# Layer 3's recurrence: the product with B moves into a PSUM bank, directly ahead of the sum that takes it

## The chip, the cores and the metric

The kernel runs on one core of a Trainium2 chip. A core has five engines with an instruction queue each: TensorE (PE; its weight loads are listed as PEld), VectorE (DVE), ScalarE (ACT), GpSimd (POOL) and SyncE (SP), which here issues nearly all transfers. They share the on-chip memory SBUF; PSUM, in eight banks of 128 partitions x 512 floats, takes the products of TensorE, and VectorE and ScalarE read and write it too. Engines wait for each other, and for transfers, on semaphores. The metric is the device time of one execution in microseconds (us), the median of several runs.

## The reference

Four layers follow one another: a four-way Mamba block over 2 x 4096 tokens, two attention layers, and layer 3, a small Mamba block with a group norm. Only layer 3 changes. It cuts the 128 channels of each of the 2 x 4096 pixels into a sequence of 8 tokens of 16 channels, and runs one Mamba block over all the sequences:

```python
xz = seq @ in_proj_w.T                      # seq: (8192, 8, 16) -> 2 x 32 inner channels
xi, z = split(xz);  xs = silu(causal_conv4(xi) + conv_b)
dt, Bm, Cm = split(xs @ x_proj_w.T)         # 1, 16 and 16 columns
dt = softplus(dt @ dt_proj_w.T + dt_proj_b)
dA  = exp(dt[..., None] * A)                # (n, 8, 32, 16)
dBx = dt[..., None] * Bm[:, :, None, :] * xs[..., None]
def step(h, (dA_t, dBx_t, C_t)):
    h = dA_t * h + dBx_t                    # eight steps, one for each token
    return h, einsum('nds,ns->nd', h, C_t)
y = (ys + xs * D) * silu(z);  out = y @ out_proj_w.T
```

A group norm, a SiLU and a residual sum over the picture follow. The line that matters is `h = dA_t * h + dBx_t`: for each token one product with the state and one sum, on 32 x 16 values for each pixel.

## The kernel before

Layers 0 to 2 are the same in both kernels. In layer 3 the pixels are taken in 16 chunks of 512 (`Chunk3`, 8 for each picture). Tokens are taken in pairs: step k = 0 to 3 of a chunk holds the tokens 2k and 2k+1, called o = 0 and 1. The state of one token is a tile of 128 x 4 x 512 floats (32 inner channels x 4 states on the partitions, four groups g of states beside each other), and nearly every operation on it takes a half of it, 128 x 1024 floats. So m01 stands for the product of o = 0, half 1.

For one token and half these operations are made:

- `load` brings B to SBUF, as the tile D, by broadcast from a row tensor in HBM; SP issues it two steps ahead. Six D tiles rotate.
- `rx_` spreads dt * x ("dtx", the tile e) over the partitions with one matmul into a PSUM bank named rx.
- `db_` multiplies D by it in place, on VectorE: D = B dtx. In PLAN this is "D", made for the next step.
- `da_` makes A = exp(dt * A) on ScalarE, one step ahead.
- `mul` (m) multiplies A by the state of the token before, on POOL.
- `add` adds it to D, on VectorE (v) or POOL (g). D then is the state. The first token's state is D alone.
- `hc_` (C) multiplies A by the spread of C, which `pc_` put into a PSUM bank q with two matmuls (two q tiles of two banks each), on VectorE, for the step before; `y_` sums it over the states on TensorE, into the bank y. The share of B dtx in C h is made apart, by `cbx_` and `ecb_`; `yg_` is the gating.
- `time` makes the step size and dtx of the next chunk, two POOL operations.

The order of the work is written out by hand. The loop runs over steps s, and in each over four groups. `PLAN[k][g]` lists the operations of a group, in the order in which each engine gets its own; `prepare` issues the `pc_` of the following C at the head of a group that has a C, `y_` and the entries of `first` come next, and the entries of `extra` behind the plan's. Every engine takes its instructions in the order in which they are issued here. Before the change both `rx_` of a step are entries of `extra`, at the end of the step two ahead, into two banks.

A chunk has 14 m, 14 D, 8 v, 4 g and 14 C. In PSUM, layer 3 holds the banks misc (1), rx (2), q (4) and y (1).

Of the kernel before, what the change touches and what calls it, by code (L numbers as in the profile page):

```python
# [7 lines left out]
F32 = mybir.dt.float32  # L8
# [5 lines left out]
P = 128  # L14
B, C, H, W = 2, 128, 64, 64
L = H * W
T = 512
# [34 lines left out]
def _bc(ap, axis, shape):  # L52
    return ap.unsqueeze(axis).to_broadcast(shape)
# [3 lines left out]
def conv_seq_kernel(ctx: ExitStack, tc: tile.TileContext, a: dict, out: bass.AP):  # L57
    nc = tc.nc
# [8 lines left out]
    x = gt([P, B, L], "x")  # L67
# [30 lines left out]
    with ExitStack() as c0:  # L98
# [3 lines left out]
        ps = c0.enter_context(tc.tile_pool(name="ps0", bufs=1, space=PSUM))  # L102
# [380 lines left out]
        nk = len(chunks)  # L483
# [12 lines left out]
        with tc.manual_schedule():  # L496
            c, c1 = chunks[:2]
# [113 lines left out]
            for k, c in enumerate(chunks):  # L611
# [8 lines left out]
                A, V, M, G = {}, {}, {}, {}  # L620
# [191 lines left out]
    with ExitStack() as c1:  # L812
# [7 lines left out]
        ps = c1.enter_context(tc.tile_pool(name="ps1", bufs=1, space=PSUM, reuse_waits="tile"))  # L820
# [301 lines left out]
        for n, j in enumerate(jobs):  # L1122
# [67 lines left out]
        with tc.manual_schedule():  # L1190
# [22 lines left out]
            for slot in range((len(groups) + 2) * UPG):  # L1213
                u = slot % UPG
                G = at(slot)[0]
# [5 lines left out]
                G, d = at(slot - 1)  # L1221
# [4 lines left out]
                G = at(slot - UPG)[0]  # L1226
# [34 lines left out]
    with ExitStack() as c3:  # L1261
# [15 lines left out]
        class Chunk3:  # L1277
# [104 lines left out]
            def rx_(self, k, o):  # L1382

                if k == 3 and o:
                    return
                i, j = PLACE[k]
                r = slice(32 * (j + o), 32 * (j + o) + 32)
                q = self.rx[k, o] = ps.tile([P, T], F32, tag="rx", name="rx", bufs=2)
                mm(q, lhsT=rep[r, :], rhs=self.e[r, i, :], start=True, stop=True)

            def db_(self, k, o, half):
                d = self.D[k, o][:, 2 * half : 2 * half + 2, :]
                nc.vector.tensor_mul(d, d, _bc(self.rx[k, o], 1, [P, 2, T]))

            def da_(self, k):

# [12 lines left out]
                a_ = self.A[k, o][:, g, :]  # L1409
                nc.gpsimd.tensor_mul(a_, a_, h)  # L1410

            def add(self, k, o, half, eng):
                g = slice(2 * half, 2 * half + 2)
                d = self.D[k, o][:, g, :]
                eng.tensor_add(d, d, self.A[k, o][:, g, :])  # L1415

            def unit(self, k, u):

# [105 lines left out]
        def prepare():  # L1524
# [8 lines left out]


        PLAN = (
# [4 lines left out]
        )  # L1540


        y = ps.tile([P, T], F32, tag="y", name="y")

        with tc.manual_schedule():
# [3 lines left out]
            c.spread(0)  # L1549
            for o in range(2):  # L1550
                c.load(0, o)
            for o in range(2):
                c.rx_(0, o)
            c1.xs = xs1
            c1.dt_(0)
            norms = [Norm(b) for b in range(B)]
            for s in range(-1, len(steps) + 3):
# [12 lines left out]
                def more(key, *what, at=extra):  # L1570
                    at.setdefault(key, []).extend(what)
# [28 lines left out]
                if n2 is not None:  # L1600
                    more((k, 0), lambda: n2.spread(n2k), lambda: n2.load(n2k, 0))
                    more((k, 1), lambda: n2.load(n2k, 1))
                    more((k, 3), lambda: n2.rx_(n2k, 0), lambda: n2.rx_(n2k, 1))
                if ci == NCH:
                    more((3, 2), nrm.first)
                    more((3, 3), nrm.second, nrm.third)
# [8 lines left out]
                        more(at_, lambda j=j: nrm.store(j, (G, V)[j % 2]))  # L1615

                nd = 0
                for g in range(4):
                    ops = PLAN[k][g].split()
                    if pc_ is None:  # L1620
                        ops = [o for o in ops if o != "C"]
                    if nc_ is None:
                        ops = [o for o in ops if o != "D"]
                    if cc is None:
                        ops = [o for o in ops if o[0] not in "mvg"]
                    if "C" in ops:
                        prepare()


                    if pc_ is not None and pk and g:  # L1630
                        pc_.y_(pk, g - 1)
                    (older, ok) = at(s - 2)
                    if g == 0 and older is not None and ok:
                        older.y_(ok, 3)
                    for f_ in first.get((k, g), []):
                        f_()
                    if g == 0 and nc_ is not None:
                        nc_.da_(nk)
                    for o in ops:
                        if o == "C":  # L1640
                            c_, k_, u_ = cs[used]
                            c_.hc_(k_, u_)
                            used += 1
                        elif o == "D":
                            nc_.db_(nk, nd // 2, nd % 2)
                            nd += 1
                        elif o == "time":
                            if fut is not None:
                                fut.dt_add()
                                fut.dtx_()  # L1650
                        elif o[0] == "m":
                            cc.mul(ck, int(o[1]), int(o[2]))
                        else:
                            cc.add(ck, int(o[1]), int(o[2]), V if o[0] == "v" else G)
                    for f_ in extra.get((k, g), []):
                        f_()
                if s < 0:
# [120 lines left out]
```

## Time and profile before

| what | value |
|---|---|
| median of three runs | 6480.78 us (6466.40 to 6482.95) |
| the profiled execution | 6465.86 us, span 6464.1 us |
| VectorE / POOL / TensorE / ScalarE busy | 5684.0 / 5442.7 / 5753.8 / 4459.6 us |
| layer 3, 5700 to 6464 us | VectorE 709.7, POOL 635.6, TensorE 657.0, ScalarE 363.1 us |
| VectorE's sum of layer 3 (L1415), 128 of them | 2298 ns each |
| POOL's product (L1410), 224, and sum (L1415), 64 | 2370 and 2895 ns each |
| VectorE's product B dtx (L1393), 224 | 1210 ns each |

The page counts an instruction as busy from its start to its end, so that an instruction that started and could not get on is busy too. A profiled group is written as line, engine, operation, out<-in, shape and count. In a timeline the columns are start, length, engine, line and operation, "x2" means that two follow each other directly, and the idle time before it stands in brackets, with the instruction or transfer that ended it. TensorE's matmuls in float32 are recorded in passes, so that one pair of `pc_` shows as four records, and their ends are modelled.

### The profile page before, as it was taken

To read this page: it belongs to the slowest core of one execution; us is meant where nothing else is said; L and a number is where in the kernel's file an instruction comes from. 1 tells how busy PE (TensorE), PEld (TensorE's weight loads), DVE (VectorE), ACT (ScalarE), POOL (GpSimd) and SP (SyncE) were. 2 spreads that over 40 slices of the span, in tenths; PEclk is the share of its full clock that TensorE was granted. 3 is DMA by queue.
4 is the path that set the end of the run, shared out by engine and by line. 5 is a ranking of instruction groups with operands and counts; after the bars stand their busy time and mean duration, and the time that the engine had idled before them with its cause. 6 is when DMAs were issued, how large, how long until landed. Compare 5 with 4: busy or idle time off the path is not lost.

```text
span 6464.1 us, 66100 instructions
## 1 busy us (share of the span) xinstructions
PE 5753.8 (89%) x19758; PEld 2749.6 (43%) x19758; DVE 5684.0 (88%) x4604; ACT 4459.6 (69%) x7643; POOL 5442.7 (84%) x2543
## 2 busy tenths in 40 slices
PE   8888888888888888888888999999999999888897
PEld 2222222222222222222224888888888888222222
DVE  7999999999999999999998777777777777899998
ACT  7887778877788777888776566556556565554543
POOL 6999999999999999999997677666766566788887
PEclk8888787877778777887777999999999999789888
DMA  6566665566665656665662000000000000877775
GB/s 183 144 152 162 162 154 145 144 150 150 150 151 148 151 148 148 145 150 151 149 147 66 1 5 3 1 1 1 1 1 1 2 6 7 204 177 178 185 181 130
DMA packets 400474, 700.32 MB, mean 108 GB/s; under 512 B 74089, under 2 KB 76658, under 8 KB 399730
## 3 DMA queue, kind: packets, MB, share of 16 engines
q1 hardware_dynamic: 399232, 694.33, 43.9%
q8 instruction: 155, 2.54, 0.2%
q14 instruction: 205, 1.68, 0.1%
q10 hardware_dynamic: 882, 1.78, 0.1%
HBM read 584.53 MB, written 111.28 MB: 108 GB/s over the span
## 4 chain that ended last, share of the span: by engine, by line
PE 39%; POOL 16%; DMA 14%; DVE 11%; ACT 10%; issue 8%; SPq 3%; POOLq 0%; DVEq 0%; ACTq 0%
PE s L961 13%; PE av L1016 12%; POOL dbu L383 9%; DVE h L427 4%; DMA D<-rows 4%; POOL hc L437 3%; DMA dus<-ddu 3%; ACT da L396 3%; PE misc L281 2%; DVE hc L439 2%; DMA cs<-rows 2%; DMA dts<-ddt 2%; PE y L450 2%; PE misc L1076 1%; DVE D L1415 1%
## 5 line engine op out<-in xcount | busy, mean ns | idle before, releaser
L383 POOL TENSOR_TENSOR dbu<-dus,bs 128x1024 f32<-128x1024 f32 x1024 | 2461.5, 2441 | 104.9 <-DVE h L427 87.2
L427 DVE TENSOR_TENSOR_SCAN h<-da,hst,dbu 128x1024 f32<-128x1024 f32 x896 | 2094.6, 2345 | 95.5 <-ACT dbu L411 87.7
L396 ACT ACTIVATE da<-dts,aneg 128x512 f32<-128x512 f32 (+1 forms) x2048 | 1410.4, 689 | 352.4 <-DVE h L427 313.7
L1004 POOL TENSOR_TENSOR sum<-sum,sc 128x1024 f32<-128x1024 f32 x378 | 897.6, 2375 | 397.2 <-ACT sc L999 392.4
L966 ACT COPY sc<-s 128x512 f32<-128x512 f32 x1024 | 596.9, 585 | 704.2 <-PE s L961 576.3
L961 PE MATMUL s<-q,k 128*128 128x256 f32 x4096 | 1053.9, 380 | 10.0 <-ACT lo L919 5.5
L450 PE MATMUL y<-hc,cst 128*32 128x512 f32 x4096 | 877.0, 753 | 207.8 <-DVE hc L439 187.8
L1016 PE MATMUL av<-sc,v 128*128 128x256 f32 x4096 | 1051.1, 380 | 9.1 <-ACT sc L999 9.1
L973 DVE TENSOR_TENSOR mx<-mx,s 128x512 f32<-128x512 f32 x896 | 609.9, 681 | 370.3 <-ACT sc L966 362.6
L439 DVE TENSOR_TENSOR hc<-h,pc 128x1024 f32<-128x1024 f32 x704 | 845.3, 1201 | 10.3 <-PE y L450 8.4
L961 PEld LDWEIGHTS s<-q,k 128*128 128x128 f32 x4096 | 772.3, 191 | 124.5 <-issue 8.3
L1016 PEld LDWEIGHTS av<-sc,v 128*128 128x128 f32 x4096 | 772.7, 190 | 116.4 <-ACT sc L999 14.4
L437 POOL TENSOR_TENSOR hc<-h,cs 128x1024 f32<-128x1024 f32 x320 | 763.1, 2385 | 1.1 <-issue 1.1
L416 PE MATMUL pc<-xd,sel 16*128 16x512 f32 x1024 | 707.0, 781 | 0.1
L1410 POOL TENSOR_TENSOR A<-A,D 128x1024 f32<-128x1024 f32 x224 | 526.6, 2370 | 139.6 <-DVE D L1415 109.8
L996 DVE TENSOR_TENSOR sc<-sc,pm 128x1024 f32<-128x1024 f32 x512 | 620.7, 1212 | 1.7 <-PE pm L991 1.7
L999 ACT ACTIVATE sc<-sc 128x1024 f32<-128x1024 f32 x512 | 543.3, 1061 | 43.3 <-DVE sc L996 43.1
L340 PE MATMUL misc<-xd,w_dt 9*128 9x512 f32 x504 | 369.9, 821 | 143.9 <-ACT x L479 77.1
L450 PEld LDWEIGHTS y<-hc,cst 128*32 128x32 f32 x4096 | 125.2, 120 | 863.2 <-DVE hc L439 427.3
L411 ACT ACTIVATE dbu<-hst,dbu,df 128x1 f32<-128x1 f32 x896 | 337.9, 377 | 84.3 <-POOL dbu L383 61.8
L1427 PE MATMUL q<-xs,room 32*128 32x512 f32 x840 | 283.5, 687 | 70.3 <-DVE A L1433 69.1
L416 PEld LDWEIGHTS pc<-xd,sel 16*128 16x128 f32 x1024 | 182.3, 218 | 350.6 <-issue 303.2
(315 smaller groups left out, 7728.0 us busy)
## 6 DMA issues: line engine op xcount, KB each, us to landing
dts<-ddt SPq DMA_DIRECT2D x512, 256.0 KB, 5.4
dus<-ddu SPq DMA_DIRECT2D x512, 256.0 KB, 5.0
D<-rows SPq DMA_DIRECT2D x448, 256.0 KB, 5.9
bs<-rows SPq DMA_DIRECT2D x1024, 64.0 KB, 4.9
cs<-rows SPq DMA_DIRECT2D x1024, 64.0 KB, 3.2
ddt<-dt SPq DMA_DIRECT2D x128, 256.0 KB, 2.0
ddu<-dtu SPq DMA_DIRECT2D x128, 256.0 KB, 4.0
dtr<-ddt SPq DMA_DIRECT2D x448, 64.0 KB, 2.0
```

The lines of the kernel that those rows point to most:

```text
L383: nc.gpsimd.tensor_mul(t, self.dus[q], _bc(self.bs[g], 1, [P, 2, T]))
L396: act(t[:, i, sl], self.dts[q][:, i, sl], AF.Exp, scale=an[:, g, 2 * q + i : 2 * q + i + 1])
L416: mm(t, lhsT=sel[32:48, 4 * g : 4 * g + 4, :].rearrange("p n d -> p (n d)"), rhs=self.xd[32:48, :], start=True, stop=True)
L427: nc.vector.tensor_tensor_scan(ho, ai, bi, init, ALU.mult, ALU.add)
L437: nc.gpsimd.tensor_mul(t, self.h[u], _bc(self.cs[gq(u)[0]], 1, [P, 2, T]))
L439: nc.vector.tensor_mul(t, self.h[u], _bc(self.pc[u // 2], 1, [P, 2, T]))
L450: mm(self.y[q // 2][r : r + 32, :], lhsT=sum4, rhs=self.hc[u][:, i, :], start=False, stop=(u % 8 >= 6), skip_group_check=True)
L961: mm(p[:, o, :], lhsT=j.k[m // 8][:, m % 8 * P : m % 8 * P + P], rhs=self.q, start=True, stop=True)
L973: nc.vector.tensor_max(self.mx, self.s[0][:, 0:2, :] if u == 1 else self.mx, self.p[u])
L996: nc.vector.tensor_sub(s, s, _bc(self.pm[:, :], 1, [P, 4, NQ]))
L1004: self.adds.tensor_add(self.sum, self.s[0] if w == 1 else self.sum, self.s[w])
L1016: mm(self.av, lhsT=self.job.v[m // 8][:, m % 8, :], rhs=self.s[u // 2][:, m % 4, :], start=(m == 0), stop=(m == 31))
```

## The change

Eight of the fourteen B dtx products of a chunk leave their place one step ahead. In the new `fuse` (x in PLAN) VectorE makes the product for one group of 512 columns into a new PSUM bank "dd", and then the sum, which takes it from there and A from SBUF and writes D; this twice for a half. The fuse stands where v stood. Of the six other products, the four whose sum is POOL's (d) now stand in the same step, directly behind x10 (in step 3: at the head of the second group), and the two of the first token stay one step ahead (D).

rx has one bank in place of two; the other one is dd. A table `RX` gives for each rx matmul the step and group at whose head, behind `prepare` and `y_`, it is issued.

```diff
-                q = self.rx[k, o] = ps.tile([P, T], F32, tag="rx", name="rx", bufs=2)
+                q = self.rx[k, o] = ps.tile([P, T], F32, tag="rx", name="rx")
...
+            def fuse(self, k, o, half):
+                d, a_ = self.D[k, o], self.A[k, o]
+                for g in (2 * half, 2 * half + 1):
+                    t = ps.tile([P, T], F32, tag="dd", name="dd")
+                    nc.vector.tensor_mul(t, d[:, g, :], self.rx[k, o])
+                    nc.vector.tensor_add(d[:, g, :], t, a_[:, g, :])
...
         PLAN = (
-            ("m10 m11 C D", "C D time", "C v10 D", "g11 D C"),
-            ("m00 m01 C D v00", "C v01 D m10 m11", "v10 D", "g11 D"),
-            ("m00 m01 C D v00", "C v01 m10 m11", "C v10 D", "g11 C"),
-            ("m00 m01 C D", "C v00 D g01 m10 m11", "C D", "D C"),
+            ("m10 m11 C", "x10 d11 C", "time C", "g11 C"),
+            ("m00 m01 C x00", "x01 m10 m11 C", "x10 d11", "g11"),
+            ("m00 m01 C x00", "x01 m10 m11 C", "C x10 d11", "C g11"),
+            ("m00 m01 C x00", "d01 g01 m10 m11 C", "C D", "D C"),
         )
+        RX = {(0, 0): (0, 1), (0, 3): (1, 0), (1, 2): (1, 1), (1, 3): (2, 0), (2, 2): (2, 1),
+              (2, 3): (3, 0), (3, 2): (0, 0)}
...
-            for o in range(2):
-                c.rx_(0, o)
...
-                    more((k, 3), lambda: n2.rx_(n2k, 0), lambda: n2.rx_(n2k, 1))
...
+                for (rk, g), (to, o) in RX.items():
+                    c_ = cc if to == k else nc_
+                    if rk == k and c_ is not None:
+                        first.setdefault((k, g), []).insert(0, lambda c_=c_, to=to, o=o: c_.rx_(to, o))
...
-                            nc_.db_(nk, nd // 2, nd % 2)
+                            nc_.db_(nk, 0, nd)
...
+                            do = {"x": cc.fuse, "d": cc.db_, "g": cc.add}[o[0]]
+                            do(ck, int(o[1]), int(o[2]))
```

More of the change, by code (lines that the diff above doesn't have):

```diff
@@ L1410, in mul, with add @@
                 nc.gpsimd.tensor_mul(a_, a_, h)
-            def add(self, k, o, half, eng):
+            def add(self, k, o, half):
                 g = slice(2 * half, 2 * half + 2)
                 d = self.D[k, o][:, g, :]
-                eng.tensor_add(d, d, self.A[k, o][:, g, :])
+                nc.gpsimd.tensor_add(d, d, self.A[k, o][:, g, :])
             def unit(self, k, u):
@@ L1624, in conv_seq_kernel @@
                     if cc is None:
-                        ops = [o for o in ops if o[0] not in "mvg"]
+                        ops = [o for o in ops if o[0] not in "mxdg"]
                     if "C" in ops:
@@ L1653, in conv_seq_kernel @@
                         else:
-                            cc.add(ck, int(o[1]), int(o[2]), V if o[0] == "v" else G)
+                            do = {"x": cc.fuse, "d": cc.db_, "g": cc.add}[o[0]]
+                            do(ck, int(o[1]), int(o[2]))
                     for f_ in extra.get((k, g), []):
```

## The prediction

> **What bounds the kernel now.** I read the busy table first, then the stages by windows, then the groups of layer 3, and last the timelines of POOL and VectorE over one chunk. The page's head says how large the whole is, and the windows of two chunks of layer 3 say that no engine is full there:
>
> ```profile
> span 6464.1 us, 66100 instructions
> ...
> 5864.80:5977.20 112.40, 99.89 (x318) 26.19 (x316) 108.91 (x86) 57.19 (x64) 98.84 (x42) 0.91 0.78 179
> ```
>
> Over these 112.4 us VectorE counts 108.9 busy and POOL 98.8. The groups of layer 3 (columns: line, engine, operation; busy us, mean ns; idle time before and who ended it) show that VectorE's figure is not all work:
>
> ```profile
> L1410 POOL TENSOR_TENSOR A<-A,D 128x1024 f32<-128x1024 f32 x224 | 526.6, 2370 | 139.6 <-DVE D L1415 109.8 <-DMA dtr<-ddt 27.3 <-DMA D<-rows 2.6
> L1415 DVE TENSOR_TENSOR D<-D,A 128x1024 f32<-128x1024 f32 x128 | 294.1, 2298 | 4.0 <-POOL A L1410 3.3
> ...
> L1433 DVE TENSOR_TENSOR A<-A,q 128x1024 f32<-128x1024 f32 x224 | 268.6, 1210 | 3.8 <-PE q L1427 3.8
> L1393 DVE TENSOR_TENSOR D<-D,rx 128x1024 f32<-128x1024 f32 x224 | 268.5, 1210 | 38.4 <-PE q L1427 24.0 <-DMA D<-rows 12.7 <-DMA dtr<-ddt 1.7
> ```
>
> All three VectorE groups have the same shape. Those with an operand in PSUM take 1.21 us; the add with both operands in SBUF takes 2.30. The timeline of POOL over a clean chunk (start us, length us) says why:
>
> ```profile
> 5929.57 4.66 POOL L1410 TENSOR_TENSOR A<-A,D 128x1024 f32<-128x1024 f32 x2
> 5935.39 2.35 POOL L1410 TENSOR_TENSOR A<-A,D 128x1024 f32<-128x1024 f32 x1 [1.17 <-DVE D L1415]
> 5939.05 2.35 POOL L1410 TENSOR_TENSOR A<-A,D 128x1024 f32<-128x1024 f32 x1 [1.31 <-DVE D L1415]
> 5941.47 3.22 POOL L1415 TENSOR_TENSOR D<-D,A 128x1024 f32<-128x1024 f32 x1
> 5944.65 4.68 POOL L1410 TENSOR_TENSOR A<-A,D 128x1024 f32<-128x1024 f32 x2
> ...
> 5959.63 4.70 POOL L1410 TENSOR_TENSOR A<-A,D 128x1024 f32<-128x1024 f32 x2
> 5964.40 2.35 POOL L1415 TENSOR_TENSOR D<-D,A 128x1024 f32<-128x1024 f32 x1
> 5967.92 9.32 POOL L1410 TENSOR_TENSOR A<-A,D 128x1024 f32<-128x1024 f32 x4 [1.16 <-DVE D L1415]
> ...
> 5985.29 2.39 POOL L1410 TENSOR_TENSOR A<-A,D 128x1024 f32<-128x1024 f32 x1
> ```
>
> POOL works at 2.34 us an operation, 20 a chunk (14 products, 4 sums, two for the step size), 46.8 us. Each of VectorE's eight SBUF sums stops it for about 1.16 us, as an idle gap or as a 3.22 in place of 2.35. POOL and that sum never run together, and this pair sets the pace. Token step by token step (k=1: 5929.57 to 5944.65; k=2: to 5959.63; k=3: to the first product of k=0, 5967.92 + 4.65; k=0: to 5985.29) the chunk costs 15.1 + 15.0 + 12.9 + 12.7 = 55.7 us.
>
> **The change, part by part.** *POOL, ScalarE and SP* keep their instructions in their order; no DMA moves. POOL's 46.8 us stay.
>
> *The eight SBUF sums of a chunk* become a fuse: twice a product of 512 into the new bank and a sum that takes it from there. Eight of the fourteen products B dtx move with them, from one step ahead to directly ahead of the sum. No operation of a fuse has two SBUF operands. The rows nearest to them (1.21 us with POOL at work) say that POOL no longer stops: up to 8 x 1.16 = 9.3 us a chunk gained. The product's row is y<-e,misc (PSUM out), the sum's is sz<-sz,y, both 0.7 us. But each operation now needs the one before it on its own engine. The trace has one pair of that kind:
>
> ```profile
> 5906.84 0.68 DVE L1448 TENSOR_TENSOR sz<-sz,y 128x512 f32<-128x512 f32 x1
> 5907.62 0.70 DVE L1379 TENSOR_TENSOR y<-e,misc 128x512 f32<-128x512 f32 x1
> 5908.23 1.22 DVE L1433 TENSOR_TENSOR A<-A,q 128x1024 f32<-128x1024 f32 x1
> ```
>
> L1379 writes what L1448 reads, and starts 0.78 after it; L1433 depends on neither, and starts 0.61 after L1379. So a fuse lasts 3 x 0.78 + 0.68 = 3.02 us, 2.94 to the next start, where product and sum had 1.13 + 1.13 of work. At 0.60 throughout it would be 2.48. I take 0.78, since that row has the dependence.
>
> The Trainium skill, "VectorE: DVE Perf Modes", section "The DRAIN you can't avoid", says that eight copies with a semaphore after each took as long as with one at the end, and advises fewer operations rather than fewer semaphores. By its first half the spacing would be 0.60 and the sum below +29 us; its second half speaks against this change; the row differs from the first half.
>
> *What now lies between POOL's operations.* g11 (POOL's sum of a step) waits for m11, and now also for d11, a product that stands last on VectorE. Before, that product was a step early. I walk k=1 from the start of m00; a hand-over costs 0.07. VectorE after m00's end (2.36): the first fuse from its sum on, 0.78 + 0.78 + 0.60 = 2.16; yg 0.78; ecb 0.60; fuse x01 2.94; C 1.13; fuse x10 2.94; d11 1.21. That is 11.76, in which POOL has three products, 7.0. So g11 starts at 2.36 + 0.07 + 11.76 + 0.08 = 14.27 and k=1 lasts 16.6: **+1.5**.
>
> k=2: no yg and ecb, but a second C, and x01 stands directly behind x00 (0.18 more): 2.16 + 3.12 + 1.13 + 1.13 + 2.94 + 1.21 = 11.69. Here the single bank of rx adds a wait. Its matmul for x10 stands on TensorE behind the pc pair of its group, which needs the q bank that the C before has just left, and behind a y group. That is 1.06 + 1.06 + 0.6 to 0.7 after that C's end, while VectorE has one C of 1.13 to do: 1.7 of waiting. Sum 13.4, k=2 lasts 18.2: **+3.2**.
>
> k=3: g01 waits for d01, behind x00, yg0 and ecb1: 2.16 + 0.78 + 0.60 + 1.21 = 4.75, against 2.34 of POOL work; the step lasts 2.43 + 4.75 + 0.08 + 3 x 2.34 = 14.3: **+1.4**. k=0: x10 and d11 fit beside m11 and the two step-size operations; five operations of 2.34: 11.7, **-1.0**.
>
> *Other moves at nothing.* Two rx matmuls at a time become seven single ones, no more in number; their other waits (rx for x01's successor in k=1, for k=3, for k=0) fall beside one to three operations of VectorE that are already queued, and cost up to 1 us a step each if TensorE is late. D's loads are needed a step later, which can give back the 12.7 us that products waited for them. Where POOL waits today for other things (stalls of 2.6 to 3.7 us in about four chunks, and the norm's loads) the new waits lie under the old: about -12 us.
>
> **Sum**: 16 x (1.5 + 3.2 + 1.4) - 15 x 1.0 = +83; less 12, about **+70 us**. The profiled execution took 6465.9 us (span 6464.1), 15 below the median of the three runs, 6480.8. So 6536 for an execution like the profiled one, **6551** beside the median.
>
> **The rivals.**
> *Dependence costs nothing* (0.60 throughout). k=1 loses 1.44, k=2 1.6, k=3 0.36 of the figures above: 16 x (0.1 + 1.6 + 1.0) - 15 = +28, less 12: 6497. For it: only one pair of rows says 0.78. Against: it repeats at 5710, 5823, 5851.
> *TensorE falls cold.* In k=1 it stands at rx for k=2 until d11 ends, some 4 us. Today's idle before a group shows the price:
>
> ```profile
> 5890.30 2.08 PE L1427 MATMUL q<-xs,room 32*128 32x512 f32 x4 [1.91 <-DVE A L1433]
> 5892.30 1.93 PE L1443 MATMUL y<-A,cst 128*32 128x512 f32 x6
> ...
> 5899.48 1.13 PE L1427 MATMUL q<-xs,room 32*128 32x512 f32 x4
> ```
>
> Behind an idle stretch the same pair takes 2.08, later 1.13. If pc, y and rx of k=2 run cold, 2.5 more each chunk: 16 x 2.5 = 40, 6591; against it stands the work between, some 9 us, that warms it. The Trainium skill, "TensorE: Matmul & The Clock Gate", section "Part 1: The HAM clock gate", gives about 3.4 us of idling for the fall to half rate, by which this case would be the likelier.
> *Faster: POOL is freed and no wait takes the stop's place.* Then VectorE's own work bounds: 8 x 2.94 + 6 x 1.13 + 14 x 1.13 + 4.0 = 50.1 a chunk, 5.6 less, 16 x 5.6 = 90: 6391. It decides where the stretch from m00's end to g11 falls below 10.2 us in k=1 and k=2; I have 11.8 and 13.4. Partial forms end between 6391 and 6480.
> *It doesn't do what it says*: if the fuse's sums were still held by POOL, each would wait out one more product, over 1 us x 16 sums a chunk: above 6700. The 1.21 us rows speak against it.
>
> **How the numbers follow.** Main case 0.52, no cost of dependence 0.16, cold TensorE 0.14, faster 0.08, waits that overlap to within 0.3% of the time before 0.07, held sums 0.03. 0.3% (19 us) is about what a measurement of this kernel tells from no change. The first rival's 6497 lies near that bound; of its 0.16 I give 0.03 to the same side. So slower 0.82, same 0.10, faster 0.08. The range from 6486 to 6608 leaves out the faster case, most of the same, and the held sums; the main case alone spans 6525 to 6580.
>
> **What would show it.** Right: VectorE's 128x1024 SBUF sum gone, POOL's g11 at 2.35 rather than 3.22, a fuse near 3.0 us, POOL's largest idle ended by VectorE's D product ahead of the sums of k=1 and k=2 (2.9 and 5.6 us), VectorE waiting on rx in k=2. Wrong: POOL idle under 8 us a chunk, k=1 and k=2 at or under 15 us, or fuses longer than 3.5 us.

## The result and the profile after

The changed kernel took **6725.79 us** (median of four executions, 6721.69 to 6736.18), the kernel before 6475.73 on the same chip: a ratio of **1.0388** (95% interval 1.037 to 1.0405), 250 us slower. The forecast had the direction and most of the places, but only 70 of the 250 us, and its range ended at 6608.

The page of the profile after begins so:

```profile
span 6720.5 us, 66576 instructions
```

All of the excess lies in layer 3: POOL's first step-size operation there starts at 5521.6 us before and at 5522.3 after, its last at 6332.0 and 6564.5. The windows from 5700 to 6400 us, the first line from the kernel before, the second from after (columns: the window, its length, busy us of PE, PEld, DVE, ACT and POOL, then TensorE's granted clock, the DMA share, GB/s):

```profile
5700.00:6400.00 700.00, 614.09 (x1906) 157.56 (x1904) 663.32 (x522) 347.69 (x387) 603.41 (x246) 0.89 0.78 180
```
```profile
5700.00:6400.00 700.00, 609.26 (x1482) 149.94 (x1482) 472.70 (x560) 271.45 (x304) 443.38 (x192) 0.75 0.60 139
```

VectorE and POOL are idle far more; TensorE is as busy as before with a fifth fewer instructions, at a granted clock of 0.75 in place of 0.89. The groups of layer 3 after (busy us, mean ns, then the idle time before them and who ended it):

```profile
L1417 POOL TENSOR_TENSOR A<-A,D 128x1024 f32<-128x1024 f32 x224 | 525.4, 2363 | 160.4 <-DVE D L1400 128.4 <-ACT A L1407 18.8 <-issue 13.0
...
L1399 DVE TENSOR_TENSOR dd<-D,rx 128x512 f32<-128x512 f32 x256 | 177.8, 694 | 175.1 <-PE rx L1389 160.2 <-DMA D<-rows 6.5 <-DMA dtr<-ddt 3.4
...
L1389 PE MATMUL rx<-e,cst 32*128 32x512 f32 x210 | 157.8, 840 | 100.2 <-DVE D L1393 87.0 <-DVE dd L1399 13.2
L1422 POOL TENSOR_TENSOR D<-D,A 128x1024 f32<-128x1024 f32 x64 | 151.0, 2359 | 274.3 <-DVE D L1393 156.8 <-issue 67.9 <-DMA D<-rows 38.3
L1393 DVE TENSOR_TENSOR D<-D,rx 128x1024 f32<-128x1024 f32 x96 | 115.2, 1213 | 51.5 <-PE rx L1389 49.3 <-PE q L1434 2.2
```

The same rx group of the kernel before:

```profile
L1389 PE MATMUL rx<-e,cst 32*128 32x512 f32 x210 | 82.5, 706 | 2.8 <-DVE D L1393 2.8
```

A ring of waits is to be seen. VectorE stands idle 160 + 49 = 209 us for rx, and TensorE 100 us at rx for VectorE, which must first have read the one bank; before, TensorE waited 2.8. POOL stands 274 us ahead of its sums, nearly all of it for the product d (what is put down to "issue" or a long finished load has the same place).

POOL's timeline over one chunk (start, length; in brackets the idle time before and what ended it):

```profile
5914.03 2.35 POOL L1417 TENSOR_TENSOR A<-A,D 128x1024 f32<-128x1024 f32 x1 [2.74 <-DVE D L1400]
5918.35 2.36 POOL L1417 TENSOR_TENSOR A<-A,D 128x1024 f32<-128x1024 f32 x1 [1.96 <-DVE D L1400]
5923.51 2.35 POOL L1422 TENSOR_TENSOR D<-D,A 128x1024 f32<-128x1024 f32 x1 [2.81 <-DMA D<-rows]
...
5942.83 2.35 POOL L1422 TENSOR_TENSOR D<-D,A 128x1024 f32<-128x1024 f32 x1 [6.92 <-DVE D L1393]
...
5954.24 2.35 POOL L1422 TENSOR_TENSOR D<-D,A 128x1024 f32<-128x1024 f32 x1 [4.42 <-issue]
...
5979.97 2.37 POOL L1422 TENSOR_TENSOR D<-D,A 128x1024 f32<-128x1024 f32 x1 [6.53 <-DVE D L1393]
```

These are m10 (2.74), m11 and g11 of k=1, g11 of k=2 (6.92), g01 of k=3 (4.42) and g11 of k=0 (6.53). From such timelines I took the gap ahead of each POOL operation, and the length of a chunk as the distance from one step-size operation to the next, over 13 chunks (the distance at the change of picture is left out). Before: 56.9 us on average. After: **73.2** (65.7 to 87.3); that is POOL's 46.8 of work and 26.5 of gaps. The forecast's walk gave 60.8, with 14.0 of gaps.

Who makes VectorE wait is seen on TensorE in the same chunk:

```profile
5939.38 1.06 PE L1450 MATMUL y<-A,cst 128*32 128x512 f32 x6
5942.75 1.62 PE L1389 MATMUL rx<-e,cst 32*128 32x512 f32 x2 [2.32 <-DVE D L1393]
5944.30 2.08 PE L1290 MATMUL misc<-xs,room 128*128 128x512 f32 x2
5946.31 2.08 PE L1434 MATMUL q<-xs,room 32*128 32x512 f32 x4
...
5959.90 2.07 PE L1389 MATMUL rx<-e,cst 32*128 32x512 f32 x2
...
5973.63 2.07 PE L1389 MATMUL rx<-e,cst 32*128 32x512 f32 x2
...
5984.79 1.05 PE L1450 MATMUL y<-A,cst 128*32 128x512 f32 x4
```

After an idle 2.32 us every matmul takes twice as long, until about 5984, 40 us without another gap; the granted clock of that stretch is 0.50. In it TensorE is what everybody waits for, and VectorE's timeline shows each rx coming later:

```profile
5938.62 0.70 DVE L1399 TENSOR_TENSOR dd<-D,rx 128x512 f32<-128x512 f32 x1 [2.91 <-PE rx L1389]
...
5962.01 2.35 DVE L1393 TENSOR_TENSOR D<-D,rx 128x1024 f32<-128x1024 f32 x2 [5.64 <-PE rx L1389]
...
5975.74 0.70 DVE L1399 TENSOR_TENSOR dd<-D,rx 128x512 f32<-128x512 f32 x1 [8.42 <-PE rx L1389]
```

### The profile page after: what moved, and what is told of

It reads as the page before. It is cut to its first block, busy times and chain, and to the rows that moved or that the text cites. A ratio compares the mean times of both kernels' runs of the same rounds, so it can differ in the third digit from the quotient of the medians.

```text
span 6720.5 us, 66576 instructions
## 1 busy us (share of the span) xinstructions
PE 5986.9 (89%) x19758; PEld 2799.3 (42%) x19758; DVE 5611.4 (83%) x4860; ACT 4458.5 (66%) x7643; POOL 5400.7 (80%) x2543
## 4 chain that ended last, share of the span: by engine, by line
PE 46%; DVE 12%; POOL 12%; DMA 10%; ACT 10%; issue 8%; SPq 2%; DVEq 0%; ACTq 0%; POOLq 0%
PE s L961 12%; PE av L1016 12%; POOL dbu L383 7%; DVE h L427 4%; PE misc L281 3%; PE q L1434 3%; DMA dus<-ddu 3%; POOL hc L437 3%; DVE hc L439 3%; ACT da L396 3%; PE y L1450 2%; PE misc L1290 2%; PE rx L1389 2%; PE y L450 2%; DMA dts<-ddt 1%
## 5 line engine op out<-in xcount | busy, mean ns | idle before, releaser
L1434 PE MATMUL q<-xs,room 32*128 32x512 f32 x840 | 342.2, 777 | 37.8 <-DVE A L1440 37.7
L1422 POOL TENSOR_TENSOR D<-D,A 128x1024 f32<-128x1024 f32 x64 | 151.0, 2359 | 274.3 <-DVE D L1393 156.8
```

## The experiments

Where no interval is given, a time is of one execution, beside the kernel before in the same set (6455 to 6473; 6476 beside the changed kernel); so differences under some 20 us are not read, and between two sets each run is taken against its own kernel before.

**Is it TensorE's idle time?** Zero-weight matmuls fill TensorE's idle time ahead of the blocked rx of k=2 and k=3:

```diff
+            def fill(self, n):
+                for _ in range(n):
+                    mm(y, lhsT=none, rhs=x[:, 0, 0:T], start=False, stop=False, skip_group_check=True)
...
+                        if (k, g) in ((1, 3), (2, 3)):
+                            first[k, g].insert(0, lambda c_=c_, n=5 - k: c_.fill(n))
```

> The changed kernel, with four matmuls by a tile of zeros added to the bank y ahead of the rx matmul at group 3 of step 1, and three ahead of that at group 3 of step 2, where TensorE stands idle for VectorE's last product (the sum in y is unchanged; TensorE has some 6 to 7 us more work a chunk at the full clock). Theory 'clock' (the idle time makes TensorE fall to half rate, and the half-rate matmuls then hold VectorE): the granted clock over layer 3 rises from 0.76 to 0.88 or more and the time falls by 80 to 200 us from the changed kernel's 6726, although work was added. Theory 'chain' (the late product d11 behind two fuses on VectorE holds POOL, whatever the clock): no fall, 0 to +100 us.

**6792.27 us**, 66 slower than after (78 if each is taken against its own kernel before). TensorE's idle time ahead of rx fell from 100 to 9 us, but its clock stayed at 0.75, so that this did not test the rate: it fell at other gaps instead. TensorE's timeline:

```profile
5878.43 1.06 PE L1454 MATMUL y<-A,cst 128*32 128x512 f32 x4 [1.76 <-DVE y L1379]
5880.68 2.08 PE L1438 MATMUL q<-xs,room 32*128 32x512 f32 x4 [1.20 <-DVE A L1444]
5882.69 1.92 PE L1454 MATMUL y<-A,cst 128*32 128x512 f32 x4
...
5907.33 1.13 PE L1438 MATMUL q<-xs,room 32*128 32x512 f32 x4
```

**Is it the one bank?** The kernel before, with one bank for rx and nothing else of the change; each rx goes to the head of the group that uses it, behind `prepare` and `y_`, as in the change:

```diff
-                q = self.rx[k, o] = ps.tile([P, T], F32, tag="rx", name="rx", bufs=2)
+                q = self.rx[k, o] = ps.tile([P, T], F32, tag="rx", name="rx")
...
+                    for g, o in ((0, 0), (2, 1)):
+                        first.setdefault((k, g), []).insert(0, lambda o=o: nc_.rx_(nk, o))
```

> The kernel before, with one bank for rx in place of two and each rx matmul issued at the head of group 0 and group 2 of the step before its products' use; products, sums and their places are those of before. If the single bank alone brings TensorE into step with VectorE: +100 us or more over the kernel before and a clock under 0.80 in layer 3. If the bank hurts only together with the products moved behind the sums' input (theory 'chain'): within 40 us of the kernel before.

**6630.30 us**, +166 without fuse and without a single moved product. VectorE, which before the change has no wait for rx in its row, now has:

```profile
L1393 DVE TENSOR_TENSOR D<-D,rx 128x1024 f32<-128x1024 f32 x224 | 269.3, 1214 | 247.7 <-PE rx L1389 228.4 <-DMA D<-rows 11.1 <-DMA dtr<-ddt 4.5
```

So the larger part of the loss comes with the bank and its rx. Whether by the lost bank itself or by where the rx now stands is left open by this run.

**The order on VectorE, and rx later.** First d11 ahead of x10 (in all three steps), then rx behind y0, sz and dt at two places:

```diff
-            ("m10 m11 C", "x10 d11 C", "time C", "g11 C"),
+            ("m10 m11 C", "d11 x10 C", "time C", "g11 C"),
...
```

> The changed kernel, with d11 ahead of the fuse x10 in steps 0, 1 and 2, so that POOL's sum g11 no longer waits for that fuse. Theory 'chain': each g11 of steps 1 and 2 starts 2.9 us earlier, 16 x 2 x 2.9 = 94, time 6610 to 6650. Theory 'clock': the rx of the next step is still held until the last product of x10, about as late as before, TensorE stays slow and the time moves by less than 40 us (above 6685).

```diff
-                        first.setdefault((k, g), []).insert(0, lambda c_=c_, to=to, o=o: c_.rx_(to, o))
...
+                        if (k, g) in ((1, 3), (2, 3)):
+                            first.setdefault((k, g), []).append(f_)
```

> The changed kernel, with the rx matmuls at group 3 of steps 1 and 2 issued behind the other matmuls of that group's head (y0 and sz, or dt) instead of ahead of them, so that TensorE has 1 to 2 us of work while it would stand. Theory 'clock': idle time ahead of rx falls by half, the clock rises above 0.80, time falls by 60 us or more, to 6665 or less. Theory 'chain': within 20 us of 6726.

**6762.09** and **6745.19 us**: neither brought the gain that one of its two theories expected. With d11 first, d11 itself waits for the late rx: VectorE's waiting now stands ahead of L1393 (243 us, 220 of it for rx; 35 ahead of the fuse), and the clock is 0.69. With rx this late VectorE's order did not help. The later rx cost little (19 us, 31 against its own kernel before); that TensorE's queue is late there anyway would explain it, but is not shown.

**The forecast's chain without rx.** One rx matmul in the whole layer; all products and fuses read that bank:

```diff
+                if not once:
+                    once.append(ps.tile([P, T], F32, tag="rx", name="rx"))
+                    mm(once[0], lhsT=rep[r, :], rhs=self.e[r, i, :], start=True, stop=True)
+                self.rx[k, o] = once[0]
```

> The changed kernel with a single rx matmul at the start of layer 3 and none after it: all products take that one bank (what is left out is the spread of dtx for every later token, so the output is not the reference's). Everything else is as in the changed kernel. Theory 'just in time' (with one bank the rx matmul cannot run before the last product has read the bank, then stands in TensorE's queue, and the two engines wait for each other): most of the 250 us goes, 6480 to 6560, clock in layer 3 above 0.84. Theory 'chain' (fuse and d11 on VectorE hold POOL by themselves): 6650 or more.

**6542.15 us**, +81. For k=1, k=2 and k=0 POOL's gaps are those of the walk: m11 of k=1 1.9, its g11 2.8, m11 of k=2 0.7, its g11 3.9 (the walk without its rx term: about 4), no gap at k=0. At k=3 they are not: g01 waits 4.5 us on average, where the walk has 2.6. VectorE's gating and `ecb_`, which stand ahead of d01, wait there for TensorE:

```profile
5859.94 0.69 DVE L1457 TENSOR_TENSOR sz<-sz,y 128x512 f32<-128x512 f32 x1 [1.68 <-PE y L1452]
5861.66 0.70 DVE L1379 TENSOR_TENSOR y<-e,misc 128x512 f32<-128x512 f32 x1 [1.03 <-PE misc L1290]
```

A chunk takes 60.6 us, where the walk without its rx term has 59.1; the forecast's sum without that term is +43, not +81. The rest of the changed kernel's 250 us, 169, comes with the rx matmuls.

**Two banks for rx.** PSUM has no bank left, so the q tiles became three of one bank in place of two of two; the kernel before with the same q is its comparison:

```diff
-                q = self.q[k, u] = ps.tile([P, 2, T], F32, tag="q", name="q", bufs=2)
+                q = self.q[k, u] = [ps.tile([P, T], F32, tag="q", name="q", bufs=3) for _ in range(2)]
```

> The changed kernel with two rx banks again, each rx matmul issued two or three groups ahead of its use; the bank for it comes from q, which has three tiles of one bank in place of two tiles of two, and C is two operations of 512. The fuse and the places of the products are those of the changed kernel. Beside 'beforeq3'. 'Just in time': 0 to 70 us above 'beforeq3', POOL waiting for d11 by about 3 us in steps 1 and 2 as the prediction's walk has it. 'Chain' as the main cause: 150 us or more above.

> The kernel before with q as three tiles of one bank and C as two operations of 512, nothing else: the price of that way of making room. VectorE has 14 x 0.07 us more a chunk, and a matmul of pc can be at most three ahead instead of four: 0 to 60 us above the kernel before under both theories.

**6675.06** and **6618.33 us**. Between them lie only 57 us, less than the 81 of the chain: with two banks, and rx issued two or three groups ahead, VectorE's fuse waits 4.5 us for rx in all, in place of 160. The pair is no clean price, since its comparison kernel is slow itself: one bank less for q, with C in two operations, costs the kernel before 157 us, with TensorE at a clock of 0.75 and waiting 71.5 us for VectorE to leave q. There VectorE waits 96.6 us for rx, although it has two banks.

**The fuse itself.** The old operations (product in place, SBUF sum) at the new places, one bank:

```diff
-                for g in (2 * half, 2 * half + 1):
-                    t = ps.tile([P, T], F32, tag="dd", name="dd")
-                    nc.vector.tensor_mul(t, d[:, g, :], self.rx[k, o])
-                    nc.vector.tensor_add(d[:, g, :], t, a_[:, g, :])
+                self.db_(k, o, half)
...
+                nc.vector.tensor_add(d, d, self.A[k, o][:, g, :])
```

> The changed kernel with the operations of before in the new places: where the fuse stood, the product in place (128x1024, PSUM operand) and directly behind it VectorE's sum from SBUF; one rx bank and its table as in the changed kernel. 'Just in time': the single bank stays, 6640 to 6760. If the four chained operations of the fuse were the cause: 6480 to 6560.

**6739.09 us**, 13 above after (28 if each is taken against its own kernel before). The PSUM sum, which is what the change is named for, is worth little here: POOL's gaps come to about 26 us a chunk in both.

**The place of rx in TensorE's queue.** After, with each rx at the head of its group ahead of `pc_` and `y_`, and that for k=1 a group earlier; one bank as in the change:

```diff
...
+                    for f_ in ahead.get(g, []):
+                        f_()
                     if "C" in ops:
                         prepare()
```

> The changed kernel with each rx matmul issued at the head of its group ahead of the pc pair and the y group, and that for x00 of step 1 one group earlier, as soon as its bank can be free; the bank, the fuse and the plan stay. Theory 'just in time' (rx comes late because it stands behind pc and y, and behind them at half clock): POOL's gaps before m10 of step 1 (4.2 us on average), before g11 of step 2 (8.4) and of step 0 (2.1) fall to 0, 4 to 5 and 0, 10 to 12 us a chunk: 6520 to 6580. If the bank's coupling itself is what costs (TensorE stands for VectorE's last product wherever rx is issued): above 6660.

**6551.71 us**, +96 over its own kernel before in place of +250: 154 us come back, without a bank. VectorE's waits for rx fall from 209 to 63 us, the clock is 0.86, a chunk takes 61.6. That is near the chain without rx (+81, 60.6). That the time equals the forecast's 6551 is chance: this set's kernel before took 6455, the forecast counted from 6481.

TensorE's own waiting did not shrink: it stands 108 us at rx, after 100, and ahead of k=2's rx as long as in after (3.73 us):

```profile
L1389 PE MATMUL rx<-e,cst 32*128 32x512 f32 x210 | 147.8, 790 | 108.3 <-DVE D L1393 92.4 <-DVE dd L1399 16.0
...
5970.81 2.07 PE L1389 MATMUL rx<-e,cst 32*128 32x512 f32 x2 [3.73 <-DVE D L1393]
```

But the half rate behind that gap and behind the next, of 2.32 us, lasts 10.2 and 6.8 us by the granted clock; in the chunk of after shown above it lasts 6.8 us behind the gap of 3.73 and 41 behind that of 2.32. So it was not these gaps that went.

**And then the order on VectorE.** The same, with d11 ahead of x10, and d01 ahead of x00:

> As 'rxhead', and with the product of POOL's sum first: d11 ahead of the fuse x10 in steps 0, 1 and 2, d01 ahead of the fuse x00 in step 3. 'Just in time' plus the walk of the prediction: g11 of steps 1 and 2 and g01 lose 2.8, 2.9 and 2.5 to 4 us of waiting, 8 to 9 a chunk: 130 us below 'rxhead' if nothing else turns late, 60 to 100 below as I expect since VectorE has 50 us of work in a chunk: 6440 to 6500. If TensorE's standing is the bound: no fall, as in 'dfirst'.

**6479.56 us**, +24, a chunk of 57.6. The order that lost 36 us while rx came late (48 against its own kernel before) gains 72 where it comes early.

**The y sums left out**, which take a good third of TensorE's records in a chunk, after and before:

```diff
             def y_(self, k, u):
+                return
```

> The changed kernel without the matmuls of y_ (the sum of C h over the states is left out, so the output is not the reference's): 14 us of TensorE's 50 us of work at full clock in a chunk are gone, and with them the entry that stands between pc and rx. If the wait for rx is so long because TensorE is nearly full at the clock it gets: 40 to 100 us above 'noybefore', like 'norx'. If the wait does not come from TensorE's load: 180 us or more above.

> The kernel before without the matmuls of y_, to go beside 'noyafter'. POOL's and VectorE's shared pace bounds it under both theories: 6420 to 6465.

**6624.42** and **6473.85 us**: 151 apart in place of 250. About 100 us hang on the y sums, by TensorE's load or by their place ahead of rx; this pair does not part the two. The kernel before at a clock of 0.65 keeps its pace (57.1 a chunk): with rx issued a step ahead and a third less to do, a slow TensorE costs it nothing.

**One bank, rx early, nothing else.** The counterpart of the run with one bank: rx at the head of the group ahead of `pc_` and `y_`:

```diff
...
+                    if nc_ is not None and g in (0, 2):
+                        nc_.rx_(nk, g // 2)
                     if "C" in ops:
                         prepare()
```

> The kernel before with the two products and all sums as they were, but one bank for the spread of dtx; each spread of dtx now goes to TensorE at the head of the group of operations that uses it, ahead of that group's C products and y sums (the run with one bank before had it behind them and took 6630.3). Theory P (the place of the spread in TensorE's queue costs, the lost bank as such does not): 6460 to 6530, VectorE waits under 60 us for rx. Rival B (a single bank costs by itself, wherever the spread stands): 6590 or more, VectorE waits over 120 us for rx.

**6485.03 us**, +12, against 6630.30, +166, with rx behind `pc_` and `y_`. VectorE's product is not listed as waiting for rx; TensorE now stands 99 us at rx, where in the slow counterpart it stood 25:

```profile
L1393 DVE TENSOR_TENSOR D<-D,rx 128x1024 f32<-128x1024 f32 x224 | 268.6, 1211 | 94.5 <-PE q L1427 61.9 <-DMA D<-rows 27.7 <-DMA dtr<-ddt 4.6
L1389 PE MATMUL rx<-e,cst 32*128 32x512 f32 x210 | 144.9, 775 | 99.2 <-DVE D L1393 99.2
```

The lost bank as such costs under 20 us; what costs is an rx that stands behind work of its own group. TensorE's waiting at rx is no measure of the loss, VectorE's is.

**Lateness without a falling rate.** The version with rx at the head, with three zero-weight matmuls ahead of it in five groups:

```diff
+                    if cc is not None and (k, g) in ((0, 2), (1, 2), (1, 3), (2, 2), (2, 3)):
+                        cc.fill(3)
                     for f_ in ahead.get(g, []):
                         f_()
```

> The version with the spread at the head of its group (6551.7), plus three matmuls with a weight of zeros into y (0.53 us each at the full rate, 1.6 together) ahead of the spread in five of the chunk's groups. It measures what lateness alone costs while TensorE has more to do, not less. Theory P: each late spread moves VectorE's fuse or product by up to 1.6 us; the places where POOL waits for them at all (k=1's x10, k=2's x00 and x10, k=3's product) are four, so up to 6.4 us a chunk, 95 us in all: 6600 to 6660, POOL's gaps at m10_1 and g11_2 up by 1 to 2 us each. Rival T (the place did not matter, only the idle time that it gave TensorE): more work for TensorE ahead of the spread leaves the time at 6530 to 6570.

**6588.99 us**, between the two expectations: 37 above the run without the extra matmuls, or 20 if each is set against the kernel before of its own set (6455 and 6473). The three matmuls took 2.7 to 2.8 us together, and not the expected 1.6, which counted one record for a matmul of two. TensorE's clock rose from 0.86 to 0.95, and both things are seen in POOL's gaps: those of k=1 grew (m10 by 3.3 us, g11 by 1.0), those of k=2 and k=3 shrank (g11 by 0.7, g01 by 1.3).

**What bounds what is left.** From the version of 6479.56, small moves: VectorE's two operations on y and TensorE's output projection later, x00 ahead of C in k=1.

```diff
-            ("m00 m01 C x00", "x01 m10 m11 C", "d11 x10", "g11"),
+            ("m00 m01 x00 C", "x01 m10 m11 C", "d11 x10", "g11"),
...
-                    more((1, 0), lambda: old.yg_(1))
+                    more((1, 1), lambda: old.yg_(1))
...
-                    more((1, 0), lambda: cc.ecb_(0))
+                    more((1, 1), lambda: cc.ecb_(0))
...
-                    more((1, 1), lambda: fut2.xs_(0), at=first)
+                    more((1, 1), lambda: fut2.xs_(0))
...
-                    more((2, 1), old.xr_, at=first)
+                    more((2, 2), old.xr_)
```

> The version with the spread at the head of its group and the product ahead of the sum it is not needed for (6479.6), with four small moves taken from its gaps on POOL (1.5 at m10_1, 2.0 at m11_1, 3.35 at g11_2): VectorE's two operations on y in k=1's first group go a group later (1.4 us ahead of the first sums), the C product behind the first sums of k=1 (1.2), and TensorE's output projection behind the spread of k=2 (1.9). If POOL's chain sets the time, it shortens by 3 to 5 us a chunk: 6405 to 6440, which would be faster than before by some 0.5%. If TensorE's clock or another engine sets it, 6460 to 6490.

**6505.99 us**, ratio 1.0047 (1.003 to 1.0064): not the gain expected. The gaps aimed at went (m10 of k=1 from 1.5 to 0, g11 of k=2 from 3.3 to 1.7), but one of 5.4 came at g11 of k=1: an input projection (misc) waits for VectorE's y, which is now later, and the rx of that g11 stands behind it. So these projections went behind that rx, and in a second version VectorE's y operations one group later still:

```diff
-                    more((1, 1), lambda: fut2.xs_(0))
-                    more((1, 2), lambda: fut2.xs_(1), at=first)
+                    more((1, 2), lambda: fut2.xs_(0), lambda: fut2.xs_(1), at=first)
```

> As the last version, but the input projection of the chunk after next no longer stands ahead of the spread of k=1's second half on TensorE (there it waits 3.05 us for VectorE's y, since both use the one misc bank, and the spread waits behind it; POOL's gap at g11_1 is 5.6 us). It follows the spread instead. If the place in TensorE's queue is what costs, g11_1 falls to 1 to 2 us, four us a chunk come back, 60 us in all: 6430 to 6460, faster than before. If not, 6490 or more.

> As best4, with VectorE's two operations on y (1.4 us) one group later still, behind k=1's second product and sum, and the input projections behind k=2's spread. If VectorE's chain to g11_1 is what is left there, g11_1 is under 0.5 us and the time 10 to 25 us under best4: 6415 to 6450. If the later y operations hold TensorE (its y sums and the misc bank wait for them), it is slower than best4.

**6514.33** (ratio 1.008, 1.0062 to 1.0098) and **6537.16 us** (1.0117, 1.0091 to 1.0142). The gap at g11 of k=1 fell from 5.4 to 1.3, as expected, and to 0.1; but the time did not follow, since g11 of k=2 took over: 5.3 and 8.7 on average, and in two sizes. In the first of the two versions three chunks take 55 us and ten 61.4 to 62.4, with the same instructions in the same order. Windows of two long chunks and a short one:

```profile
5632.60:5695.00 62.40, 58.70 (x159) 15.13 (x158) 48.51 (x59) 28.65 (x32) 46.89 (x20) 0.78 0.80 186
5817.90:5879.35 61.45, 57.76 (x159) 14.93 (x158) 48.54 (x59) 28.65 (x32) 46.91 (x21) 0.81 0.71 160
5577.20:5632.60 55.40, 50.98 (x159) 13.44 (x158) 48.36 (x59) 28.66 (x32) 46.85 (x21) 0.91 0.95 233
```

VectorE, ScalarE and POOL are equally busy in all three; what differs is TensorE's clock, and the DMA, which is busier in the short chunk. The half rate begins at the projection that waits for y, and there TensorE could be given something to do: in the first of these two versions, two zero-weight matmuls are added to the rx that stands ahead, in its own bank, which nobody needs yet.

```diff
-                mm(q, lhsT=rep[r, :], rhs=self.e[r, i, :], start=True, stop=True)
+                n = 2 if (k, o) == (1, 1) else 0
+                mm(q, lhsT=rep[r, :], rhs=self.e[r, i, :], start=True, stop=not n)
+                for m in range(n):
+                    mm(q, lhsT=none, rhs=x[:, 0, 0:T], start=False, stop=m == n - 1)
```

> In the last but one version some chunks take 55 us and most take 61.4, with the same instructions; in the long ones TensorE stands idle 2.2 and 0.8 us in k=1 (it waits for VectorE's y and for ScalarE's xs) and then runs at half rate for some 15 us, and POOL waits 6.5 us at g11_2 in place of 1.5. Here two matmuls with a weight of zeros are added to the spread of k=1's second half, in its own bank (1.06 us each at the full rate), which fill the idle 2.2 us before anyone needs the bank. Theory T (the idle time drops TensorE's rate, and the rate is worth 6 us a chunk): most chunks at 55 to 57, 6420 to 6460. Rival W (the waits alone set the long chunks, the rate only goes with them): more work for TensorE cannot help, 6510 to 6530.

**6457.39 us** (ten executions), ratio **0.9976** (0.9963 to 0.999): faster than the kernel before, though by less than the 0.3% that I count as a difference. TensorE without the two matmuls, in a long chunk:

```profile
5955.92 1.02 PE L1389 MATMUL rx<-e,cst 32*128 32x512 f32 x2
5959.13 1.13 PE L1290 MATMUL misc<-x,room 128*128 128x512 f32 x2 [2.19 <-DVE y L1379]
5961.03 2.07 PE L1290 MATMUL misc<-x,room 128*128 128x512 f32 x2 [0.78 <-ACT xs L1297]
5963.04 2.07 PE L1389 MATMUL rx<-e,cst 32*128 32x512 f32 x2
```

and with them:

```profile
5924.94 1.02 PE L1390 MATMUL rx<-e,cst 32*128 32x512 f32 x2
5925.89 1.98 PE L1392 MATMUL rx<-x,none 128*128 128x512 f32 x4
5928.15 1.12 PE L1290 MATMUL misc<-x,room 128*128 128x512 f32 x2 [0.27 <-DVE y L1379]
5930.05 1.13 PE L1290 MATMUL misc<-x,room 128*128 128x512 f32 x2 [0.78 <-ACT xs L1297]
5931.40 1.12 PE L1390 MATMUL rx<-e,cst 32*128 32x512 f32 x2 [0.23 <-DVE dd L1402]
```

POOL's g11 of k=2, without and with:

```profile
5918.64 2.35 POOL L1422 TENSOR_TENSOR D<-D,A 128x1024 f32<-128x1024 f32 x1 [6.45 <-DVE D L1393]
```
```profile
5943.42 2.35 POOL L1425 TENSOR_TENSOR D<-D,A 128x1024 f32<-128x1024 f32 x1 [1.07 <-DVE D L1396]
```

The wait for ScalarE (0.78) is still there, the projection still comes when VectorE's y lets it, and yet every chunk now takes 53.7 to 56.2 us (mean 54.7, 60.1 without). TensorE has more to do and keeps its rate; nothing else is changed. So the rate by itself is worth 5.4 us a chunk in that version. Against the kernel before the chunks save 2.2 us each, 33 over 15, but the execution only 11: the stretch behind the last step-size operation takes 156 us in place of 132, at a clock of 0.72 in place of 0.84. That was not followed up.

## Why the prediction was wrong

- **POOL's work and its release: right.** g11 takes 2.36 us in place of 2.90, VectorE's SBUF sum is gone, and no fuse stops POOL. But the 9.3 us a chunk it was priced at never showed, since POOL has gaps anyway; the run with the SBUF sum at the new places is only 13 to 28 us slower.
- **The fuse at 3.02 us: right.** In VectorE's timeline after, a fuse with nothing else to wait for lasts from 5864.73 to 5867.74:

```profile
5864.73 0.69 DVE L1399 TENSOR_TENSOR dd<-D,rx 128x512 f32<-128x512 f32 x1
5865.52 0.69 DVE L1400 TENSOR_TENSOR D<-dd,A 128x512 f32<-128x512 f32 x1
5866.25 0.69 DVE L1399 TENSOR_TENSOR dd<-D,rx 128x512 f32<-128x512 f32 x1
5867.05 0.69 DVE L1400 TENSOR_TENSOR D<-dd,A 128x512 f32<-128x512 f32 x1
5867.66 2.34 DVE L1440 TENSOR_TENSOR A<-A,q 128x1024 f32<-128x1024 f32 x2
```

  Its operations start 0.73 to 0.80 us apart, the C behind them, which needs none of them, after 0.61. The rival at 0.60 does not hold for these operations with PSUM operands (and the +29 that the forecast names for it is +16 by its own terms, 6497). The Trainium skill found on eight copies that the semaphore costs nothing extra ("VectorE: DVE Perf Modes", "The DRAIN you can't avoid"); a dependence costs 0.12 to 0.19 us here. There was some luck in it: in the pair that gave 0.78 the second operation overwrites what the first has read, while in a fuse it reads what the first has written.
- **The walk between VectorE and POOL: right for k=1, k=2 and k=0, too short at k=3.** Without the rx matmuls it is met gap by gap but for g01 of k=3: 4.5 us in place of 2.6, since gating and `ecb_` wait for TensorE, a wait that the walk left out. That is 30 (16 x 1.9) of the 38 us between its +43 and the measured +81; the rest was not traced.
- **"Its matmul for x10 ... 1.06 + 1.06 + 0.6 to 0.7 ... 1.7 of waiting": the place was right, the term too small.** VectorE waits 2.9 us there even ahead of the half rate. One rx matmul is two records that start 0.53 us apart, 1.12 us together (5931.40 in the last version's lines above, at the full rate); I had taken the length of one record, 0.706 on average, for the whole matmul.
- **"Their other waits ... fall beside one to three operations of VectorE ... cost up to 1 us a step each if TensorE is late", costed at nothing: this is the step that failed.** For k=0 they are 5.6 and 8.4 us in the chunk shown. The gaps that the walk doesn't have at all, m10 of k=1, m10 and g11 of k=0, are 4.2, 1.0 and 2.1 us on average, and g11 of k=2 is 8.4 in place of 5.6; without the rx matmuls they are 0, 0, 0 and 3.9. (g01 of k=3 is 4.4 in place of 2.6 too, but as much without them.) In time: all waits for rx together stood in the forecast with 27 us (16 x 1.7), and the runs have 169 (250 with the rx matmuls, 81 without). I looked at what VectorE still had to do, and not at what stood ahead of rx in TensorE's queue. Before, rx was issued a step ahead and found its bank free; with one bank it can't be issued before VectorE has read it, and whatever of the group stands ahead of it, itself waiting for VectorE, delays it. Moving rx to the head of its group, with the one bank, gives 154 us back in the changed kernel (where one rx also goes a group earlier) and 154 in the kernel before with one bank, each run taken against its own kernel before.
- **The rival "TensorE falls cold": right in kind, far too small.** It had 2.5 us a chunk, from pc, y and rx of k=2 alone, "against it stands the work between, some 9 us, that warms it" (in the lines it read, the granted clock was at half for 6.8). The half rate stays 40 us without a gap in the chunk shown, and its price falls at k=3 and k=0. As I read it, it is no rival of the late rx but goes with it: early rx at the same gaps shortens it. The share is an estimate: the shortest chunks of after, at a clock of 0.87, take 65.7 us, the walk 60.8, the mean 73.2; so of the 12.4 missing about 5 are lateness (k=3's part among them) and 7.5 the rate and what it makes later. That the rate can cause such a loss by itself is shown by the last run; how much it causes in the changed kernel itself was not isolated, since filling TensorE's idle time there did not raise its rate.
- **The rivals "faster" and "held sums"** did not occur; VectorE counts 48 to 49 us busy in chunks of 55 to 62 us, and is not the bound there.

The layer's loss is then: the chain of the walk with k=3's wait for TensorE (+81), and rx behind `pc_` and `y_` (+154), which makes VectorE wait for it and goes with long stretches of TensorE at half its rate, in which TensorE becomes the bound of the second half of a chunk. How the 154 divide between a late rx and the half rate is not shown beyond the estimate above.

## What to carry to other kernels

When a PSUM buffer is taken away from a matmul that was issued ahead, follow that matmul in TensorE's queue: everything ahead of it in the same group is now part of the wait, so put it first (154 us here, without a bank). Look at the wait of the engine that bounds: in both pairs of runs TensorE stood at rx longer in the fast version (108 against 100 us, 99 against 25). TensorE's rate behind a gap must be priced over all of the work that follows without a gap, not over the next few matmuls (6.8 to 41 us here). Where such a gap can't be removed, two idle matmuls into a bank that nobody needs yet may pay (5.4 us a chunk here); put in front of the wanted matmul they cost more than they gave (20 to 78 us in two runs).

## What the runs showed of the hardware that I had not expected

- The half rate began in or behind idle stretches of 2.3 us (after), 1.8 us (with the first fill), 2.2 and 0.8 us (the last version without its two added matmuls) and 1.9 us (the kernel before). By the granted clock it then lasted 41.0, 27.3, 23.9 and 6.8 us, which are 12, 8, 7 and 2 times 3.41 us. The Trainium skill, "TensorE: Matmul & The Clock Gate", "Part 1: The HAM clock gate", gives about 3.4 us of idling for the fall and as much of work for the return. None of these gaps is that long, and none of these returns that short; what sets the lengths is left open by the runs.
- In one and the same program, chunks with equal instructions fall into two lengths, 55 and 61 to 62 us, with the clock (0.91 against 0.78 to 0.81); two matmuls by zeros, which kept the clock up, made all of them short.
- An rx and a q pair, which take their weights from different tiles on 32 rows each, can run beside each other: in the last version an rx starts its two records at 5945.47 and 5946.00, a q pair its four at 5945.48 and 5946.01, and both are through in the 1.1 us that either takes alone.
